# Keys and values of two elements by three float32r products, with the context split where it is turned and kept in DRAM

## The chip, the cores and the metric

The kernel runs on one NeuronCore of a Trainium2 chip. The metric is the device time of one execution in microseconds (us): before the change 1100.62 us, the median of three runs between 1100.51 and 1100.92.

## The reference, cut to what matters

The input is `x`, four elements of 512 tokens with 512 channels, and a context `ctx_2048` of the same shape. Four gated layers are applied in turn:

```
x = x + tanh(g_xattn[0]) * wkv(w, u, k=layernorm(x), v=ctx)          # a recurrence along the tokens
x = x + tanh(g_ffn[0])   * ffn(layernorm(x), w1, w2, w3)             # 1-bit weights, 8-bit activations
x = x + tanh(g_xattn[1]) * attention(layernorm(x), cond=ctx)         # 16 heads of 32
x = x + tanh(g_ffn[1])   * ternary_linear(layernorm(x), gamma, W)
```

In the attention, queries and output go through products of 8-bit integers, but keys and values do not:

```
kv   = cond @ wkv.T + bkv          # float32: 512 tokens x 512 channels, 1024 outputs, for each element
k, v = split(kv, 2)
attn = softmax(q k^T / sqrt(32));  o = attn v
```

They depend on the context and the weights alone, so they can be made for all four elements at any time before the attention.

## The kernel before, in words

**Stages.** One function, `tile_flamingo_kernel`, unrolls everything. A first part (the pools "boot" and "boot_ps") loads and prepares all weights while it runs the recurrence (`wkv_layer`, L554) and the FFN (`ffn_layer`, L694) of the first element; after about 320 us a second part runs the FFN, attention and ternary layer of the elements against each other. All that the change edits runs in the first part, or moves buffers of it.

**Order.** Generators yield after each piece of work. `line(gen, (start, end, steps), ...)` gives each generator places along an axis, `event` a single place, and `run` (L1192) always takes the generator whose next place is lowest. In the first part, `at_us(us)` counts microseconds up to 88, and `at_unit(n)` counts the sixteen (tile of 128 tokens, quarter of the hidden layer) units of the first element's FFN; four steps of `ffn_layer` make one unit. These places set the order in which the program is traced. Every TensorE instruction also gets an order edge behind the last TensorE instruction of the step before (`in_turn`, L147, `next_turn`, L156), so TensorE runs the steps in exactly this order. Instructions of the other engines and the DMA issues are ordered by the framework's planner, which takes the earliest in program order whose operands and buffers are ready by its own estimate of times. Each engine then runs its queue in order. All DMAs here are issued by SyncE (SP).

**Buffers.** A tile pool has a number of buffers for each tag; a tile of a tag waits until a buffer's former tile has been read for the last time. In the first part PSUM has two banks of tag "m" (512 float32 columns each; transposes, and the keys and values of elements one to three beyond the first few), two of "hp" (FFN up products) and four of "acc". In SBUF, tag "k_half" has two buffers, "wn" (raw weights and raw context) two, "cT" one.

**Keys and values** (class `Context`, L439). `weights` and `weights_turned` (L497) fetch the two halves of `wkv` and turn them into `wkvT`, 128 x 4 x 1024 float32. `fetch(b)` (L458) brings the context of element b, `load(b)` (L473) transposes it on TensorE in tiles of 128 tokens (`ct_ps`), copies it on ScalarE into `cT`, and for the third and fourth element stores `cT` to DRAM (`cD`, L484), from where the recurrence reads it later. `keys_values(b, tag)` (L503) makes eight groups: four key groups (128 outputs x 512 tokens: four float32 matmuls over the channel blocks into one bank), each followed by `split` (L247: ScalarE writes the float32r rounding plus bias, VectorE the rest) and a store to `kD` (L520); and four value groups (128 tokens x 512 outputs), each followed by an addition of the bias on VectorE (L535) and a store to `vD` (L537). For the third element the groups stand at units 3.8 to 9.6, for the fourth at 10 to 16; the raw context of the fourth is fetched at unit 9.0 and turned at 9.75.

**FFN unit.** `up` makes eight float32r matmuls of 512 columns into an "hp" bank (twice a unit), `gate` (tanh, L737; L738) and `gated` (L742) and `quantised` (L663) use ScalarE, VectorE and GpSimd, `gate_parts` transposes the result and splits it into float32r parts (`parts`, L682, with L688 on ScalarE and L689 on VectorE), and `down` makes eight more matmuls. Between these steps come the transposes of FFN weights (`turned`, L334) and, from unit 11, the rounding and turning of `wq`, `wp`, `wf` (L368 to L423) into `wqT`, `wpT`, `wfT`.

All matmuls are recorded with line L162 and all transposes with L165, the helpers' lines; the tile's name tells which is which.

## Time and profile before

| | |
|---|---|
| median of three runs | 1100.62 us |
| profiled execution | 1100.92 us |
| its span on the core | 1099.1 us, mean granted TensorE clock 0.963 |
| TensorE busy (matmul) | 939.7 us, 85% |
| VectorE | 831.4 us, 76% |
| ScalarE | 726.0 us, 66% |
| GpSimd | 314.1 us, 29% |
| DMA | 189.68 MB, mean 173 GB/s |

The profile is of one execution. Times of instructions are counted from the start of the span. "Busy" of TensorE counts records of matmuls, which overlap one another, so the cost of one matmul in a row of them is the distance from start to start and not its recorded length. In the groups of instructions, "out<-in" are the program's names, then come partitions x elements and the count, then the total busy time, the mean of one in ns, and the idle time before them with what ended it. In the order of time, a line has start, length, engine, line, operation, names and count, and in brackets the idle time before it and what ended that. SPq is the issuing of DMAs on SyncE.

### The profile page before, as it was taken

To read this page: it belongs to the slowest core of one execution; us is meant where nothing else is said; L and a number is where in the kernel's file an instruction comes from. 1 tells how busy PE (TensorE), PEld (TensorE's weight loads), DVE (VectorE), ACT (ScalarE), POOL (GpSimd) and SP (SyncE) were. 2 spreads that over 40 slices of the span, in tenths; PEclk is the share of its full clock that TensorE was granted. 3 is DMA by queue.
4 is the path that set the end of the run, shared out by engine and by line. 5 is a ranking of instruction groups with operands and counts; after the bars stand their busy time and mean duration, and the time that the engine had idled before them with its cause. 6 is when DMAs were issued, how large, how long until landed. Compare 5 with 4: busy or idle time off the path is not lost.

```text
span 1099.1 us, 17965 instructions
## 1 busy us (share of the span) xinstructions
PE 939.7 (85%) x6380; PEld 678.8 (62%) x6380; DVE 831.4 (76%) x1600; ACT 726.0 (66%) x1490; POOL 314.1 (29%) x311
## 2 busy tenths in 40 slices
PE   4879997998888878889998787999998999878885
PEld 2335564565557666667776465777777777656652
DVE  4976548757676789997669988877697765679977
ACT  6656755567345676667767667677685666977863
POOL 3831104422323153531215546422123321100000
PEclk8889999999998999999999999999999999989998
DMA  8178945454344673744755544566455653343411
GB/s 287 39 257 326 323 170 187 147 216 171 136 134 148 233 234 112 252 134 144 230 190 189 168 164 145 172 216 187 173 200 169 208 192 106 83 149 107 116 49 39
DMA packets 85674, 189.68 MB, mean 173 GB/s; under 512 B 12241, under 2 KB 36817, under 8 KB 74577
## 3 DMA queue, kind: packets, MB, share of 16 engines
q1 hardware_dynamic: 85584, 188.53, 51.6%
q8 instruction: 51, 0.84, 0.3%
q14 instruction: 39, 0.31, 0.1%
HBM read 148.65 MB, written 39.85 MB: 171 GB/s over the span
## 4 chain that ended last, share of the span: by engine, by line
PE 45%; DVE 24%; ACT 15%; POOL 7%; issue 7%; DMA 2%; SPq 0%; POOLq 0%; ACTq 0%; DVEq 0%
PE ff_hp L162 14%; PE ff_acc L162 6%; PE pt_ps L165 5%; PE o_ps L162 4%; PE s_ps L162 4%; ACT at_P L941 3%; DVE wk_q L632 3%; PE v_ps L162 3%; ACT at_PT L961 2%; DVE at_nm L939 2%; PE k_ps L162 2%; PE tp_ps L165 2%; DVE wk_p L626 2%; PE qr_ps L165 2%; DVE qg_i L672 1%
## 5 line engine op out<-in xcount | busy, mean ns | idle before, releaser
L162 PE MATMUL ff_hp<-wT,xp 128*128 128x512 f32 x1024 | 270.0, 407 | 3.8 <-ACT at_P L941 2.1
L162 PEld LDWEIGHTS ff_hp<-wT,xp 128*128 128x128 f32 x1024 | 194.2, 193 | 51.3 <-ACT at_P L941 3.8
L941 ACT ACTIVATE at_P<-s_ps,at_nm 128x512 f32<-128x512 f32 x256 | 174.4, 689 | 73.9 <-DVE at_nm L939 70.0
L939 DVE TENSOR_REDUCE at_nm<-s_ps 128x1 f32<-128x512 f32 x256 | 165.5, 676 | 38.0 <-PE s_ps L162 37.3
L677 POOL TENSOR_TENSOR ff_z<-qg_b,qg_s 128x512 f32<-128x512 bf16 x64 | 71.8, 1121 | 334.4 <-ACT qg_b L676 308.3
L165 PE MATMUL pt_ps<-ident,at_P 128*128 128x128 f32 x1024 | 141.1, 278 | 16.4 <-ACT at_os L981 5.4
L961 ACT COPY at_PT<-pt_ps 128x512 f32<-128x512 f32 x224 | 124.3, 595 | 39.6 <-PE pt_ps L165 38.5
L162 PE MATMUL ff_acc<-wT,hr 128*128 128x512 f32 x512 | 137.3, 409 | 4.8 <-ACT hr L688 3.0
L165 PEld LDWEIGHTS pt_ps<-ident,at_P 128*128 128x128 f32 x1024 | 113.2, 140 | 44.4 <-issue 9.1
L162 PE MATMUL s_ps<-at_kR,at_qR 128*128 128x512 f32 x256 | 97.8, 450 | 22.0 <-ACT at_P L941 14.6
L162 PEld LDWEIGHTS ff_acc<-wT,hr 128*128 128x128 f32 x512 | 92.7, 190 | 25.8 <-ACT hr L688 4.0
L737 ACT ACTIVATE ff_z<-ff_hp,coef 128x512 f32<-128x512 f32 x64 | 44.0, 687 | 46.9 <-PE ff_hp L162 44.3
L162 PE MATMUL o_ps<-at_PT,at_V 128*32 128x128 f32 x2048 | 72.2, 279 | 1.3 <-DVE hr L689 0.7
L676 ACT CAST qg_b<-qg_i 128x512 bf16<-128x512 int8 x80 | 49.3, 617 | 31.3 <-DVE qg_i L672 27.4
L742 DVE SCALAR_TENSOR_TENSOR ff_z<-ff_hp,coef,ff_z 128x512 f32<-128x512 f32 x64 | 47.6, 743 | 29.1 <-PE ff_hp L162 29.1
L162 PEld LDWEIGHTS s_ps<-at_kR,at_qR 128*128 128x128 f32 x256 | 45.6, 193 | 38.8 <-ACT at_P L941 23.7
L162 PEld LDWEIGHTS o_ps<-at_PT,at_V 128*32 128x32 f32 x2048 | 53.8, 111 | 23.8 <-issue 11.3
L738 DVE SCALAR_TENSOR_TENSOR ff_z<-ff_z,ff_hp 128x512 f32<-128x512 f32 x64 | 43.4, 678 | 31.4 <-ACT ff_z L737 29.5
L162 PE MATMUL v_ps<-wkvT,cT 128*128 128x512 f32 x128 | 60.9, 622 | 5.7 <-DVE wT L295 2.3
L162 PE MATMUL k_ps<-cT,wkvT 128*128 128x512 f32 x128 | 61.4, 631 | 2.3 <-ACT wk_k L576 1.0
L165 PE MATMUL tp_ps<-ident,ff_z 128*128 128x128 f32 x256 | 40.3, 281 | 23.2 <-ACT at_PT L961 11.0
L632 DVE RECIPROCAL wk_q<-wk_q 128x256 f32<-128x256 f32 x32 | 54.3, 1718 | 1.4 <-POOL wk_p L620 1.4
(178 smaller groups left out, 1664.3 us busy)
## 6 DMA issues: line engine op xcount, KB each, us to landing
wT<-wD SPq DMA_DIRECT2D x72, 1024.0 KB, 5.3
wn<-in_L_ffn_w_dram SPq DMA_DIRECT2D x18, 1024.0 KB, 7.2
at_kR<-kD SPq DMA_DIRECT2D x128, 128.0 KB, 3.0
at_qR<-qD SPq DMA_DIRECT2D x256, 64.0 KB, 2.3
wD<-wT SPq DMA_DIRECT2D x12, 1024.0 KB, 4.2
kD<-k_half SPq DMA_DIRECT2D x16, 512.0 KB, 2.8
qD<-at_half SPq DMA_DIRECT2D x32, 256.0 KB, 2.1
cn<-in_ctx_dram SPq DMA_DIRECT2D x8, 512.0 KB, 6.0
```

Of the source, the lines that this page charges most:

```text
L162: return in_turn(nc.tensor.matmul(*args, **kwargs))
L165: return in_turn(nc.tensor.transpose(*args))
L626: nc.vector.tensor_tensor_scan(p[:, 1:], A2, E2, 0.0, ALU.mult, ALU.add)
L632: nc.vector.reciprocal(half, half)
L676: nc.scalar.copy(qb, qi)
L677: nc.gpsimd.tensor_tensor(grouped(src), grouped(qb), s.unsqueeze(2).to_broadcast([P, NG, GS]), ALU.mult)
L737: nc.scalar.activation(z, hp, AF.Tanh, scale=coef[:, 0:1])
L738: nc.vector.scalar_tensor_tensor(z, z, 1.0, hp, ALU.add, ALU.mult)
L742: nc.vector.scalar_tensor_tensor(z, hp, coef[:, 1:2], z, ALU.mult, ALU.mult)
L939: nc.vector.tensor_reduce(nm, sp, AX.X, ALU.max, negate=True)
L941: nc.scalar.activation(lanes[k, i, t], sp, AF.Exp, bias=nm, accum_out=sums[k][:, t, i : i + 1],)
L961: made[k] = nc.scalar.copy(dst, blocks(pt))
```

## The change

For the third and fourth element, a float32 product of two float32 matrices becomes three float32r products of their parts (high x high, high x low, low x high).

- Each tile of 128 context tokens of these elements, when turned, is also written as a float32r high part (ScalarE) and the remainder (VectorE) into `c_both` (tag "k_half"), both from the same PSUM bank, and stored to DRAM (`cS`). `load` now yields after each tile. `cD` is still written.
- The weights are held as two tiles `W[0]` (keys) and `W[1]` (values). Before the new products, `split_weights` splits them: low parts into buffers whose later owners (`wqT`, `wpT`, `wfT`, `bp_b`, `swp_b`) are now allocated when they are made, high parts into two "k_half" buffers and from there by DMA over the place of `W`.
- Keys and values of these two elements are made in four halves of 256 tokens. `fetch_half` brings both parts of half a context into one buffer of tag "cT"; `half_keys_values` makes two key banks (each with two output blocks of 256 columns, 12 matmuls and one `split` a block) and two value banks (12 matmuls of 512 columns each).
- Places: element four's context is fetched at unit 3.0 (before: 9.0) and turned from 3.5 (9.75); weights are split at 3.8 and 4.6; the halves run at 5.4 to 6.6, 7.2 to 8.4, 9.0 to 10.2 and 10.8 to 12.0, each fetched 0.58 unit ahead.

The first and second element keep the float32 products. The core of the diff:

```diff
@@ class Context, load @@
             for t in range(NT):
-                self.transposed(cT[:, :, t * P : (t + 1) * P], self.cn[b][t // 2][:, t % 2, :])
+                cut = slice(t * P, (t + 1) * P)
+                pt = self.transposed(cT[:, :, cut], self.cn[b][t // 2][:, t % 2, :])
+                if b > 1:
+                    both = self.pool.tile([P, 2, D], F32R, name="c_both", tag="k_half", bufs=2)
+                    nc.scalar.copy(both[:, 0, :], pt)
+                    nc.vector.tensor_tensor(
+                        both[:, 1, :], pt, both[:, 0, :].bitcast(F32), ALU.subtract
+                    )
+                    for i in range(2):
+                        nc.sync.dma_start(
+                            out=cS[b][i, :, :, cut], in_=blocks(both[:, i, :]).bitcast(F32)
+                        )
+                yield
@@ new in class Context @@
+        def split_weights(self, i):
+            W = self.W[i]
+            high = [
+                self.pool.tile([P, 2, D], F32R, name="w_hi", tag="k_half", bufs=2)
+                for _ in range(2)
+            ]
+            for c in range(NC):
+                tag = (("wqT", "wpT"), ("wfT", ("bp_b", "swp_b")))[i][c // 2]
...
+                hi = high[c // 2][:, c % 2, :]
+                nc.scalar.copy(hi, W[:, c, :])
+                nc.vector.tensor_tensor(lo, W[:, c, :], hi.bitcast(F32), ALU.subtract)
+                self.low[i, c] = lo
+                if c % 2:
+                    yield
+            self.W[i] = self.pool.tile([P, NC, D], F32R, name="w_high", tag=f"wkvT{i}")
+            for h in range(2):
+                nc.sync.dma_start(
+                    out=self.W[i][:, 2 * h : 2 * h + 2, :].bitcast(F32),
+                    in_=high[h].bitcast(F32),
+                )
+
+        def fetch_half(self, b, h):
+            self.pair = self.pool.tile([P, 2, NC, 2 * P], F32R, name="c_pair", tag="cT")
+            cut = slice(2 * P * h, 2 * P * (h + 1))
+            for i in range(2):
+                nc.sync.dma_start(
+                    out=self.pair[:, i].bitcast(F32), in_=cS[b][i, :, :, cut]
+                )
+
+        def half_keys_values(self, b, h):
...
+            def products(out, c, w, ctx):
+                i, w = w.start // D, slice(w.start % D, w.start % D + w.stop - w.start)
+                high = self.W[i][:, c, w], ctx(hi)
+                low = self.low[i, c][:, w], ctx(lo)
+                for n, (x, y) in enumerate(((0, 0), (0, 1), (1, 0))):
+                    weight, context = (high, low)[x][0], (high, low)[y][1]
+                    pair = (context, weight) if i else (weight, context)
+                    matmul(
+                        out,
+                        lhsT=pair[0],
+                        rhs=pair[1],
+                        start=(c == 0 and n == 0),
+                        stop=(c == NC - 1 and n == 2),
+                    )
+
+            for g2 in range(0, NC, 2):
+                kp = psum_tile("k_ps", "m")
+                half = self.pool.tile([P, 2, 2, 2 * P], F32R, name="k_half", tag="k_half", bufs=2)
+                for g in (g2, g2 + 1):
+                    out = kp[:, (g - g2) * 2 * P : (g - g2 + 1) * 2 * P]
+                    for c in range(NC):
+                        products(out, c, slice(g * P, (g + 1) * P), lambda a: a[:, c, :])
+                    split(half[:, g - g2], out, self.bkc[:, g : g + 1])
+                store()
...
+                yield
+            for j in range(2):
+                t = 2 * h + j
+                vp = psum_tile("v_ps", "m")
+                for c in range(NC):
+                    products(vp, c, slice(D, 2 * D), lambda a: a[:, c, j * P : (j + 1) * P])
+                V = self.pool.tile([P, D], F32, name="V", tag="k_half", bufs=2)
+                nc.vector.tensor_tensor(V, vp, self.bv_b, ALU.add)
...
@@ the places @@
-        for b, load, over, start in ((2, 0.7, 2.0, 3.6), (3, 9.0, 9.75, 9.8)):
+        for b, load, over in ((2, 0.7, 2.0), (3, 3.0, 3.5)):
             event(at_unit(load), lambda b=b: context.fetch(b))
-            event(at_unit(over), lambda b=b: context.load(b))
+            line(late(lambda b=b: context.load(b)), (at_unit(over), at_unit(over + 0.4), 4))
+        for i, start in enumerate((3.8, 4.6)):
             line(
-                late(lambda b=b: context.keys_values(b, "m")),
-                (at_unit(start + 0.2), at_unit(start + 6.0), 8),
+                late(lambda i=i: context.split_weights(i)),
+                (at_unit(start), at_unit(start + 0.4), 3),
+            )
+        for b, h, start, end in (
+            (2, 0, 5.4, 6.6),
+            (2, 1, 7.2, 8.4),
+            (3, 0, 9.0, 10.2),
+            (3, 1, 10.8, 12.0),
+        ):
+            event(at_unit(start - 0.58), lambda b=b, h=h: context.fetch_half(b, h))
+            line(
+                late(lambda b=b, h=h: context.half_keys_values(b, h)),
+                (at_unit(start), at_unit(end), 4),
             )
```

## The prediction

> **What bounds the kernel now.** I read the page's list of groups first, to see what a key or value product costs beside a float32r product, then the stage in which the edited work runs, by windows, then the waits of TensorE in that stage, then the order of time at single places. The stage is that of the first element's FFN, in which everything that the change touches is placed: about 101 us (first ff_hp) to 317 us, sixteen units of 13.5 us.
>
> ```profile
> L162 PE MATMUL ff_hp<-wT,xp 128*128 128x512 f32 x1024 | 270.0, 407 | 3.8 <-ACT at_P L941 2.1
> ...
> L162 PE MATMUL v_ps<-wkvT,cT 128*128 128x512 f32 x128 | 60.9, 622 | 5.7 <-DVE wT L295 2.3
> L162 PE MATMUL k_ps<-cT,wkvT 128*128 128x512 f32 x128 | 61.4, 631 | 2.3 <-ACT wk_k L576 1.0
> ```
>
> The program issues 16 key and value groups of four products for each of four elements, 256 products, and 256 records are here: 128 of each kind for 64 products. So one float32 product is two records. What a product costs is not its mean (records overlap) but the distance between starts, which the order of time gives:
>
> ```profile
> 115.80 2.07 PE L162 MATMUL ff_hp<-wT,xp 128*128 128x512 f32 x8
> ...
> 123.78 0.59 PE L162 MATMUL v_ps<-wkvT,cT 128*128 128x512 f32 x1
> 124.21 0.60 PE L165 MATMUL ct_ps<-ident,cn 128*128 128x128 f32 x4
> 124.41 0.69 DVE L535 TENSOR_TENSOR V<-v_ps,gamma_b 128x512 f32<-128x512 f32 x1 [2.96 <-PE v_ps L162]
> 125.16 1.09 PE L165 MATMUL ct_ps<-ident,cn 128*128 128x128 f32 x8 [0.35 <-DVE V L535]
> ...
> 133.74 3.59 PE L162 MATMUL v_ps<-wkvT,cT 128*128 128x512 f32 x8
> ```
>
> A group of v_ps is 3.59 us with the end of its last record: (3.59 - 0.59)/7 = 0.429 us a record, 0.857 us a float32 product, 3.43 us a group. For float32r, (2.07 - 0.40)/7 = 0.238 us a product of 512 columns. Transposes of 128 columns come (1.09 - 0.33)/7 = 0.109 us apart. The lines also show the wait that matters below: ct_ps stands until DVE has read the bank that it wants, and TensorE restarts 0.06 us after DVE's end.
>
> ```profile
> 101.00:317.00 216.00, 190.41 (x862) 123.84 (x861) 140.85 (x237) 128.05 (x205) 55.63 (x55) 0.98 0.53 190
> 263.00:276.50 13.50, 11.76 (x62) 7.67 (x61) 10.16 (x18) 13.16 (x23) 1.39 (x2) 1.00 0.79 289
> ```
>
> ```profile
> PE wt_ps L165 <- DVE k_half L250: 5.0, 2, 4.0
> PE wt_ps L165 <- DVE V L535: 3.9, 3, 2.7
> PE v_ps L162 <- DVE wT L295: 2.3, 2, 2.1
> ```
>
> Columns of the windows (first fence; the second is TensorE's waits in the stage: in total, times, longest): PE, PEld, DVE, ACT and POOL busy, granted clock, DMA share, GB/s. TensorE is busy 190.4 of 216 us (88%) at clock 0.98, DVE 65%, ACT 59%: TensorE bounds the stage. Its largest waits, five of the kind above, are for a PSUM bank that ACT or DVE has yet to read: the stage has two of tag "m" for all transposes, keys and values.
>
> **The change, part by part.**
>
> *Products.* Removed: 16 groups (elements three and four) x 3.43 = 54.9 us of TensorE. Added: values, 4 halves x 2 x 4 x 3 = 96 float32r products of 512 columns x 0.238 = 22.8 us; keys, 4 x 4 x 4 x 3 = 192 of 256 columns. No 256-column float32r product is in the trace. Below it is 0.109 (128 columns), above 0.238 (512). Half of 0.238 is 0.119, the straight line between the two rows gives 0.152; I take 0.130, between them and nearer the halving, since the 0.109 of the transposes is about a weight load (two came 0.108 us apart), not columns. Keys: 25.0 us (20.9 to 45.7). Sum 47.8: **-7.1 us** (-11.2 to +13.6).
>
> The row first: 0.238 us at 512 columns. The Trainium skill, TensorE: Matmul & The Clock Gate, section Back-to-back issue gap, gives N/2.4 + 2.5 ns, 216 ns at 512 columns and 109 at 256; the measurement is 10% above it. By the page the keys would take 20.9 us and the term would be -11.2.
>
> *Two key blocks in one bank.* Now each half puts two blocks of 256 columns into one PSUM tile, and the first is split (ACT, then DVE) before the second's products. No row has TensorE writing one half of a bank while another engine reads the other, so the bounds are nothing and the full wait (a wait can't gain). All of TensorE's waits on eviction in the rows are for a whole tile, so I take the full wait. It is: the last product's tail 0.40 - 0.24 = 0.16; 0.04 to start ACT (the DVE line above starts 0.04 after v_ps); ACT on 256 columns, 0.47 (L249's 0.68 at 512, less the 0.21 by which a copy falls from 0.58 at 512 to a midpoint of 0.37 with at_os's 0.27 at 128); 0.05; DVE 0.43 (line between 0.28, at_o at 128, and 0.72, L250); 0.06 to restart: 1.2 us. ACT and DVE are busy 59% and 65% with instructions of 0.7 us: half of one, in that share of cases, is 0.2 + 0.2 more: 1.6. There are 2 such pairs a half, 8 in all: **+13 us** (0 to +16). Nothing on TensorE can pass, as turns are chained: behind it queue the FFN's up and down products, and ACT and DVE wait for those.
>
> On the same point the Trainium skill, PSUM — Partial Sum Buffer, section PSUM bank collisions raise a hardware error, tells to guard by bank, not by address, disjoint columns included; no run here shows it yet, and it speaks against this change.
>
> *Loads of elements three and four.* Per tile of 128 tokens ACT gains a copy (0.59, as L688) and DVE a subtraction (0.68, as L689); the bank is held through both, 1.3 us longer. c_both has two buffers, each held by ACT, DVE, two SP issues of 0.32 and a landing (256 KB: vD<-V 2.5, at_V<-vD in 512-byte runs 4.1): 5 to 6 us, where the tiles come some 1.4 us apart. Tiles three and four wait about 2 to 3 us for a buffer with their bank held, and TensorE's next transposes stand. Per load 2 us (0 to 6): **+4 us** (0 to +12). Eight copies (4.7 us) and eight subtractions (5.4) lie otherwise beside TensorE, in ACT's and DVE's idle 41% and 35%; without that cover they would cost 10.
>
> *Queues.* SP gets 16 cS writes, 8 pair fetches, 4 weight copies, 8 more key stores: 36 issues x 0.36 = 13 us, of 216, in a queue that mostly waits (for L250 alone 68 us). The two cn fetches of element four and its cD write move from unit 9-10 to 3-4, past weight loads on SP, and take a "wn" buffer that the load of (0,2) would have had, which then comes half a unit later, about its 6.0 us landing before its use: part of the +1 below. DMA is 0.93 busy at 128-141.5 and 0.65 in the next unit, and gets about 5 MB there. POOL is passed by none of these.
>
> *Weight splits.* 8 ACT copies (0.6) and 8 DVE subtractions (0.68), no bank: hidden in the same idle shares; with slower loads **+1 us** (0 to 5). The lower parts live in the buffers of wqT, wpT, wfT, bp_b, swp_b, which are wanted from unit 12.6 and last read by 12.0: nothing, if the halves keep time. Fetches of halves: 512 KB took 5.1 us (cn); the single pair buffer leaves 0.58 unit = 7.8 us: nothing; if late by its full landing, 5 us a half. Key evictions, 16 + 16 of 256 columns for 8 + 8 of 512, +2.1 us ACT and +1.1 DVE, lie in the waits counted.
>
> *What moves.* Key and value work now ends at unit 12. In unit 12-13 (second window line) ACT is busy 13.2 of 13.5 us, so with 3.65 us of products gone it stays 13 us long: TensorE idles, **+2** (0 to 5). The windows of units 5-12 (168.5 to 263) add up to 12.9 us of TensorE idle; denser products, and the eight waits, let ACT and DVE catch up: half goes, **-6.5** (-10 to -3).
>
> Sum: -7.1 + 13 + 4 + 1 + 2 - 6.5 = +6.4. The profiled execution took 1100.92 (span 1099.1 and 1.8 around it), 0.3 above the median of 1100.62, so 1107.3 against it, 1107.0 against the median. After 320 us nothing is edited; 0.2% (2.2 us) is about what a measurement can tell from no change.
>
> **Rivals.**
> *No wait inside the bank* (ends faster): if TensorE may write columns 256-511 while ACT reads 0-255, or the waits take only time that TensorE lost anyway, 13 goes to 0 and the catching up to -3: -7.1 + 0 + 4 + 1 + 2 - 3 = -3.1, 1097.5; with the cheapest product 1093. For it: idle TensorE time exists (25.6 us). Against: each wait on a bank in the rows lasts till its last reader. It decides when a wait costs under 0.8 us net.
> *256 columns cost nearly as much as 512*: weight loads bound them; at 0.19 us the keys take 36.5, +11.5: 1118.5. For: float32r weight loads are recorded at 190 ns, transposes' at 140. Against: they overlap (0.108 apart).
> *The c_both buffers bind*: DMA at 0.9 makes landings 6 to 8 us (cD 7.0), each load costs 6: +8, 1115.
> *The stage is not the measure*: TensorE's gain and loss cancel in ACT- and DVE-bound stretches: 1098.5 to 1102.8.
>
> **How the numbers follow.** Forecast with its bounds, 1103 to 1112: 0.50. Slow product or buffers, 1112 to 1122: 0.15. Cancelling: 0.12. No wait in the bank, 1092 to 1098.4: 0.23. So slower 0.65, same 0.12, faster 0.23. Range 1094 to 1119, leaving out about 0.05 below and 0.08 above; the forecast's own is 1103 to 1112.
>
> **What would show it.** The distance of k_ps starts (0.13 at 256 columns); eight waits PE k_ps <- DVE k_half of 1 us or more, about 10 to 13 us together, where there were none; waits of ACT c_both on its DMA near 125-165 us and PE ct_ps behind; units 5.4 to 12 longer, the last four shorter; first ff_hp of the second element some 6 us later. Wrong if k_ps shows no such wait, or if the stage's TensorE idle does not grow.

## The result, and the profile after

The changed kernel takes 1134.56 us (median of four runs, 1134.38 to 1135.76); beside it the kernel before took 1100.77 (1100.51 to 1101.92). The ratio is 1.031, with a 95% interval of 1.0297 to 1.0326: 34 us slower, where the prediction had 1107.0 and a range up to 1119. The direction was right, the size was not.

First, from the groups of instructions by line and shape of the kernel after, the new key products with the high parts of the weights, of 256 columns (busy us and mean ns of one; idle time before them and what ended it).

```profile
L159 PE MATMUL k_ps<-c_pair,w_high 128*128 128x256 f32 x128 | 28.9, 320 | 28.1 <-DVE k_half L247 18.8 <-ACT w_hi L537 6.1 <-DMA c_pair<-cS 2.5
```

Half of the float32 records are gone, as announced: 64 each of k_ps and v_ps, with 33.0 and 31.9 us busy, are left of 128. But the line of the new key products has nearly as much idle time in front of it (28.1 us) as work in it, and two thirds of that is named k_half, the wait inside the bank.

Now windows of the same kernel after (PE, PEld, DVE, ACT and POOL busy, granted TensorE clock, DMA share, GB/s). The first line is the stage from the first ff_hp of the first element to the first ff_hp of the second. The others are stretches of it: the load of the third element, the 3.4 us before the longest stretch at half clock, and that stretch, from the weight splits into the first half.

```profile
100.74:367.68 266.94, 204.39 (x1069) 156.02 (x1069) 170.22 (x296) 144.42 (x238) 64.17 (x64) 0.91 0.60 205
128.00:141.50 13.50, 8.88 (x36) 6.78 (x36) 5.68 (x10) 5.86 (x9) 0.00 (x0) 0.75 0.60 177
175.80:179.20 3.40, 1.18 (x9) 0.65 (x7) 2.66 (x4) 1.11 (x2) 1.36 (x2) 1.00 1.10 423
179.20:199.70 20.50, 7.89 (x29) 6.95 (x30) 16.66 (x18) 7.69 (x13) 10.38 (x10) 0.50 0.54 181
```

The same stage of the kernel before:

```profile
100.99:332.89 231.90, 201.24 (x909) 131.40 (x908) 153.78 (x271) 133.51 (x215) 63.64 (x64) 0.98 0.54 190
```

The whole loss lies in this stage: 266.9 us instead of 231.9, +35.0. TensorE is busy 3.1 us longer and idle 62.6 us instead of 30.7, so 31.9 of the 35.0 us are idle time. Its work did not shrink in time because it ran at a lower clock: the granted clock is 0.91 instead of 0.98, so (1 - 0.91) x 266.9 = 24 us of full clock are missing, where before it was (1 - 0.98) x 231.9 = 5. Not all of that is lost time, since TensorE also stands in the slow stretches: in the one from 179.2 to 199.7 it is busy for 7.89 of 20.5 us. By the count of the products its busy time should be 8.2 us shorter (worked out further below), and it is 3.1 longer, so the lower clock costs some 11 us of busy time, an estimate. ACT has 10.9 us more work in the stage and DVE 16.4.

Where in the stage: the start of the same ff_hp matmul in both traces.

| start before (us) | 116.1 | 139.9 | 153.5 | 181.4 | 223.4 | 270.4 | 315.6 | 341.6 |
|---|---|---|---|---|---|---|---|---|
| later after by | -0.3 | 6.7 | 12.6 | 29.4 | 30.0 | 44.1 | 35.2 | 33.6 |

7.0 us are added at the load of the third element, 5.9 at that of the fourth, 17 at the weight splits and the first half, 14 at the last two halves; some 10 are won back in the last four units, and little changes after 341.6. The lags also carry products that were moved. Of the 17 us, 14.3 are idle time of TensorE; but of the 14, 9.3 are busy time, as two halves' products stand where four float32 groups stood; and what is won back comes from four value groups, 13.7 us, that have left the last units. TensorE's largest waits in the stretch from 88 to 360 us of the kernel after:

```profile
PE k_ps L159 <- DVE k_half L247: 18.8, 8, 7.9
PE tp_ps L162 <- DVE c_both L492: 6.5, 2, 4.6
PE k_ps L159 <- ACT w_hi L537: 6.1, 1, 6.1
PE wt_ps L162 <- DVE hr L800: 5.0, 4, 3.3
PE k_ps L159 <- DMA c_pair<-cS: 2.5, 4, 1.1
```

Eight waits on the first block's split were announced, and eight are there. But they range up to 7.9 us. The order of time of the kernel after shows the longest of them and the wait ahead of it (POOL, loads of weights and some other lines are left out):

```profile
175.85 2.52 SPq L554 DMA_DIRECT2D c_pair<-cS  x2
...
176.58 0.40 PE L162 MATMUL wt_ps<-identb,sg 128*128 128x128 bf16 x4
...
183.11 0.55 PE L159 MATMUL k_ps<-c_pair,w_high 128*128 128x256 f32 x1 [6.14 <-ACT w_hi L537]
...
187.92 0.47 ACT L246 ACTIVATE k_half<-k_ps,bkc 128x256 fp32r<-128x256 f32 x1 [1.86 <-DMA w_high<-w_hi]
...
189.19 2.27 DVE L737 TENSOR_TENSOR_SCAN wk_p<-wk_e 128x512 f32<-128x512 f32 x1 [1.15 <-POOL wk_e L733]
...
191.38 3.33 DVE L743 RECIPROCAL wk_q<-wk_q 128x256 f32<-128x256 f32 x2
...
194.64 0.38 DVE L247 SCALAR_TENSOR_TENSOR k_half<-k_ps,bkc,k_half 128x256 fp32r<-128x256 f32 x1
...
195.07 0.79 PE L159 MATMUL k_ps<-c_pair,w_high 128*128 128x256 f32 x2 [7.95 <-DVE k_half L247]
...
200.74 0.48 PE L159 MATMUL k_ps<-c_pair,w_high 128*128 128x256 f32 x2
...
202.11 0.28 PE L159 MATMUL k_ps<-c_pair,w_lo 128*128 128x256 f32 x1
```

From 176.98 to 183.11 TensorE stands before the first key product, whose context parts were asked for from 175.85 on, behind two weight copies on SP. The profile puts this wait down to w_hi, which the product doesn't read; the two c_pair transfers land 7.3 us after their issue (median, by the profile's DMA issues of 165 to 215 us), and 175.85 + 7.3 = 183.15, which fits the end of the wait (from 175.8 to 179.2 the DMA share is 1.10). The wait that ends at 195.07 has two parts. ACT's half of the split waits 1.86 us for a k_half buffer that a weight copy still reads, 0.8 us of it after the end of the last product at 187.12. Then DVE, which needs 0.38 us for its half, first runs a scan of the recurrence, for whose operand it stands until 189.19, and two reciprocals (2.27 + 3.33 us) that stand ahead of it in its queue. TensorE goes on 0.43 us after the split's start. The last two lines carry the price of a product: twelve start between 200.74 and 202.11, (202.11 - 200.74)/11 = 0.1245 us apart. The first distance is longer than the others; the last ten, from 201.06 on, are 0.117 us apart.

### The profile page after: what moved, and what is told of

It is laid out like the page before. It is cut to its first block, busy times and chain, and to the rows that moved or that the text cites. A ratio compares the mean times of both kernels' runs of the same rounds, so it can differ in the third digit from the quotient of the medians.

```text
span 1134.0 us, 18402 instructions
## 1 busy us (share of the span) xinstructions
PE 940.2 (83%) x6510; PEld 703.6 (62%) x6540; DVE 848.6 (75%) x1624; ACT 737.1 (65%) x1514; POOL 314.4 (28%) x311
## 4 chain that ended last, share of the span: by engine, by line
PE 44%; DVE 22%; ACT 14%; issue 7%; POOL 7%; DMA 5%; SPq 0%; ACTq 0%; POOLq 0%; DVEq 0%
PE ff_hp L159 13%; PE ff_acc L159 6%; PE pt_ps L162 5%; PE o_ps L159 4%; PE v_ps L159 3%; PE s_ps L159 3%; ACT at_P L1052 3%; PE k_ps L159 3%; DVE at_nm L1050 2%; DVE wk_q L743 2%; ACT at_PT L1072 2%; PE tp_ps L162 2%; DVE qg_i L783 1%; ACT wk_e L715 1%; DVE wk_p L737 1%
## 5 line engine op out<-in xcount | busy, mean ns | idle before, releaser
L159 PE MATMUL ff_hp<-wT,xp 128*128 128x512 f32 x1024 | 273.7, 411 | 2.8 <-ACT at_P L1052 2.1
L159 PEld LDWEIGHTS ff_hp<-wT,xp 128*128 128x128 f32 x1024 | 198.5, 198 | 48.5 <-ACT at_P L1052 3.8
L159 PEld LDWEIGHTS o_ps<-at_PT,at_V 128*32 128x32 f32 x2048 | 53.4, 110 | 22.8 <-issue 10.5
L799 ACT CAST hr<-tp_ps 128x512 fp32r<-128x512 f32 x64 | 37.6, 588 | 22.9 <-PE tp_ps L162 22.5
L159 PE MATMUL k_ps<-c_pair,w_high 128*128 128x256 f32 x128 | 28.9, 320 | 28.1 <-DVE k_half L247 18.8
```

What stands on the lines that cost most here:

```text
L159: return in_turn(nc.tensor.matmul(*args, **kwargs))
L799: nc.scalar.copy(part[:, 0, :], pt)
```

## The experiments

The theory after this reading had four parts: the waits inside the bank cost about 10 us net; the loads cost 11 to 12 instead of 4; the first half comes late through SP's queue and the k_half buffers; and pauses halve the clock. The rival was that the stage has become bound by something else, so that the removal of one wait only shows the next. Each ratio is taken to the kernel before on the same chip, whose median there was 1099.95 to 1101.68 us; differences in us between kernels carry this spread.

### Waits inside the bank

> The changed kernel, with both key blocks of a bank multiplied before either is split. Theory (the second block's products wait in TensorE's order for the split of the first, and the split's VectorE half stands behind the recurrence's scans and reciprocals): the eight waits of k_ps on k_half, 18.8 us, go, and the time falls by 14 to 20 us from 1134.6, to 1115 to 1121. Rival (TensorE would have stood there anyway, since VectorE is late in these units): the idle time turns up before other transposes and products, and the time stays above 1129.

```diff
                     for c in range(NC):
                         products(out, c, slice(g * P, (g + 1) * P), lambda a: a[:, c, :])
+                for g in (g2, g2 + 1):
+                    out = kp[:, (g - g2) * 2 * P : (g - g2 + 1) * 2 * P]
                     split(half[:, g - g2], out, self.bkc[:, g : g + 1])
```

With both blocks multiplied before both splits: 1124.31 us (1123.65 to 1129.31), ratio to before 1.0221 (1.0187 to 1.0255). 10.2 us come back of the 18.8 us of these waits. Its waits from 88 to 360 us:

```profile
PE k_ps L159 <- DMA c_pair<-cS: 9.0, 3, 6.7
PE wt_ps L162 <- DVE hr L802: 8.5, 6, 3.3
PE k_ps L159 <- DVE k_half L247: 7.8, 1, 7.8
```

Seven of the eight waits are gone, 11.0 us, and the waits for hr are 3.5 us longer. The row of c_pair is longer by name only: its longest, 6.7, is the wait before the first key product, 6.1 in the changed kernel and there put down to w_hi, so it is 9.0 instead of 2.5 + 6.1 = 8.6. That the same wait has c_pair's name here speaks for the reading above. The other way to shorten the same waits is to leave them and to put the recurrence's scans, product and reciprocals behind a split that was traced before them:

> The changed kernel, with an order edge: the recurrence's scans, products and reciprocals on VectorE that are traced after a split stand behind that split's VectorE half. Nothing else is changed, the two blocks still share a bank. Theory (the long waits inside a bank are the recurrence's instructions ahead of the split in VectorE's queue): the 18.8 us of k_ps on k_half fall to 9 to 11 us (eight waits of some 1.2), and the time falls by 6 to 12 us from 1134.6, to 1122 to 1129. Rival (the recurrence is itself what the stage waits for, so that it is late instead): less than 3 us.

```diff
+        return nc.vector.scalar_tensor_tensor(
...
+                    lows.append(split(half[:, g - g2], out, self.bkc[:, g : g + 1]))
...
+            after_split(nc.vector.tensor_tensor_scan(q[:, 1:], A2, E2, 0.0, ALU.mult, ALU.add))
```

1130.72 us (1129.73 to 1133.11), ratio 1.0279 (1.0261 to 1.0297); before on that chip was 1099.95.

```profile
PE k_ps L159 <- DVE k_half L255: 10.9, 8, 2.4
PE k_ps L159 <- DMA c_pair<-cS: 9.1, 4, 6.5
...
PE k_ps L159 <- ACT wT L298: 3.4, 1, 3.4
```

The eight waits fall from 18.8 to 10.9 us and the longest from 7.9 to 2.4: so about 8 us of them were DVE's queue, and at most 1.4 us each (10.9/8) the wait itself, near the 1.6 of the prediction. But the kernel gains 3.8 us, not 8. The wait before the first key product is the same, 6.5 us, and again put down to c_pair. Other waits grow: the largest is one of 3.4 us for wT before a k_ps, where the changed kernel has 0.7.

### Where the halves and the weights stand

Three edits move the same work: the halves and their fetches one unit later; the first fetch earlier, ahead of the weight copies on SP; the weights' splits earlier, at units 0.6 and 4.0.

> The changed kernel, with all four halves and their fetches one unit later (6.4 to 13.0). Theory (the first half comes before its fetch and its split weights are there: one wait of 6.1 us and one of 0.75, with the clock at half afterwards): the wait before the first k_ps goes, and the time falls by 6 to 10 us, to 1125 to 1129; the eight waits of k_ps on k_half stay, in sum 10 to 20 us. Rival (the long waits follow from where the recurrence's instructions stand, wherever the halves are): same within 3 us.

> The changed kernel, with the first half's fetch placed at unit 3.75 (4.82), ahead of the weights' copies in SP's queue. Theory (SP stands 6.6 us at the first weight copy until VectorE has made the low part, and the fetch behind it lands only at 183 to 184 us): the 6.1 us wait before the first k_ps goes and the time falls by 4 to 7 us, to 1128 to 1131. Rival (ScalarE's split of the weights or the clock set the start of the first half): within 2 us.

> The changed kernel, with the key weights split at unit 0.6 (3.8) and the value weights at 4.0 (4.6). Theory (the weights' high parts hold both k_half buffers until their copies have landed, so that ScalarE stands at the first half's split and TensorE behind it): the 6.1 us wait before the first k_ps and the long wait (7.9 us) in the first half shrink, and the time falls by 6 to 14 us from 1134.6, to 1121 to 1128. Rival (the long waits are the recurrence's instructions ahead in VectorE's queue, or the fetch of the first half): same within 3 us.

```diff
-            (2, 0, 5.4, 6.6),
+            (2, 0, 6.4, 7.6),
...
-            event(at_unit(start - 0.58), lambda b=b, h=h: context.fetch_half(b, h))
+            event(at_unit(3.75 if start == 5.4 else start - 0.58), lambda b=b, h=h: context.fetch_half(b, h))
...
-        for i, start in enumerate((3.8, 4.6)):
+        for i, start in enumerate((0.6, 4.0)):
```

Each line of the diff was one kernel (the first with the other three halves moved alike): 1133.88 (1133.05 to 1135.07), 1139.07 (1137.17 to 1141.3) and 1142.7 us (1141.82 to 1144.33), ratios 1.0299 (1.0272 to 1.0326), 1.0353 (1.0334 to 1.0372) and 1.0376 (1.0359 to 1.0393). One changes nothing, two are slower. The theory that SP's queue or the weights' k_half buffers alone make the price of the first half fell. Where the pair is fetched first, TensorE starts the first key block 1.6 us earlier (181.46 instead of 183.11), but then its split stands 14.2 us: ACT waits 7.33 us for the k_half buffer of a weight copy, and DVE has the weights' subtractions, scans and two reciprocals ahead of its half. Its waits of this kind from 100 to 360 us:

```profile
PE k_ps L159 <- DVE k_half L247: 22.8, 8, 14.2
```

### The price of the loads

To the kernel before were added only the loads' new work, at the places that the change gives them as far as the rest of that kernel allows (units 2.0 and 9.45, in four steps); nothing reads it.

> The kernel before, with c_both made and stored for elements three and four as in the change (four steps from unit 2.0 and from 9.45), read by nothing; products as before. Theory (the price of the loads is their own, some 6 us each while DMA is at 0.85, less at unit 9.5): slower than before by 7 to 13 us, 1108 to 1114. Rival (the lag seen at the loads is only taken from slack and comes back by the end of the stage): within 3 us of the kernel before.

```diff
+                pt = self.transposed(cT[:, :, cut], self.cn[b][t // 2][:, t % 2, :])
+                if b > 1:
+                    both = self.pool.tile([P, 2, D], F32R, name="c_both", tag="k_half", bufs=2)
+                    nc.scalar.copy(both[:, 0, :], pt)
+                    nc.vector.tensor_tensor(
+                        both[:, 1, :], pt, both[:, 0, :].bitcast(F32), ALU.subtract
+                    )
+                    for i in range(2):
+                        nc.sync.dma_start(
+                            out=cS[b][i, :, :, cut], in_=blocks(both[:, i, :]).bitcast(F32)
+                        )
+                yield
```

1112.24 us (1109.75 to 1113.71), ratio 1.0095 (1.0075 to 1.0115): +10.9 us with no product changed. Two variants took the operands from the copy in SBUF, not from the PSUM bank, once here and once in the changed kernel:

> The kernel before with the loads split (as in the run of the loads alone, 10.9 us slower than before), but with c_both from the copy in SBUF. Theory (the price of the loads is the PSUM bank held while c_both waits for a buffer): 2 to 5 us slower than before, 1103 to 1106. Rival (it is ScalarE and SP standing in their queues, or DMA): 8 us or more.

> The changed kernel, with c_both made from the copy in SBUF (cT) and not from the PSUM bank, so that the bank is free after ScalarE's first copy. Theory (the two banks held while c_both waits for a buffer cost TensorE the 6.7 us of lag at the third element's load and most of the 6 us at the fourth's): the wait of tp_ps on c_both (6.5 us) goes and the time falls by 8 to 13 us, to 1121 to 1127. Rival (ScalarE itself stands in its queue at c_both until a buffer's store has landed, and all behind it stands too): it falls by less than 4.

```diff
-                    nc.scalar.copy(both[:, 0, :], pt)
+                    nc.scalar.copy(blocks(both[:, 0, :]), cT[:, :, cut])
```

Added to the kernel before: 1111.74 (1105.84 to 1113.35), ratio 1.0094 (1.0063 to 1.0125), the same price. In the changed kernel: 1130.24 (1129.47 to 1132.69), ratio 1.0269 (1.024 to 1.0297), 4.3 less than without. In the changed kernel what comes back is speed: in its stage of 260.2 us TensorE's idle time is nearly the same, 61.9 us instead of 62.6, and its busy time 6 us shorter. In the kernel before, the bank held longer is not what makes the loads' price. The order of time of the first of these two, at the third element's load (DVE, PEld and SP left out), shows what does:

```profile
132.17 0.62 ACT L487 CAST c_both<-cT 128x512 fp32r<-128x512 f32 x1 [2.90 <-DMA cS<-c_both]
...
132.69 0.58 ACT L294 CAST wT<-wt_ps 128x512 fp32r<-128x512 bf16 x1
...
133.32 0.38 PE L166 MATMUL wt_ps<-identb,sg 128*128 128x128 bf16 x4 [2.19 <-ACT wT L294]
```

ACT's third copy waits 2.90 us for a buffer that a transfer still reads. Behind it in ACT's queue stands the copy of turned FFN weights, and TensorE waits 2.19 us for that; the eight ff_acc matmuls after it, from 133.52 on, take 3.46 us, where they take 2.09 at full clock. The next three kernels take that price apart: the steps alone, the transfers alone (from `cT`; the diff is this kernel against the one with all of it), and the copies and subtractions alone.

> The kernel before with the two loads only cut into four steps and the second of them begun 0.3 unit earlier, as in the three kernels before this one: no split, no transfer. It is the zero of that comparison. If the order of the steps alone costs nothing, it is within 2 us of before; what it takes more than before is to be subtracted from the other two.

> The kernel before, with the two transfers to cS per tile of the third and fourth element issued at the places of the loads, but taken from cT itself: no copy, no subtraction, no c_both buffer. The kernel with the loads' whole new work took 10.9 us more than before, and the same with the operands taken out of SBUF 10.4. If the transfers make that price (16 more issues on the SyncE queue, 4 MB more when the DMA engines are 0.93 busy), this takes 8 to 11 us more than before. If the copies and subtractions make it, it takes 0 to 3 us more, and TensorE's waits on c_both are gone.

> The same kernel with the copy and the subtraction into c_both out of the PSUM bank, but without the transfers to cS: nothing reads c_both. If ACT's and DVE's instructions and the bank held for them make the price, this takes 8 to 11 us more than before and TensorE's waits on c_both stay (7.8 us with the transfers). If it is the transfers that hold the c_both buffers, 1 to 4 us, and those waits go to under 2 us.

```diff
-                    both = self.pool.tile([P, 2, D], F32R, name="c_both", tag="k_half", bufs=2)
-                    nc.scalar.copy(both[:, 0, :], pt)
...
-                            out=cS[b][i, :, :, cut], in_=blocks(both[:, i, :]).bitcast(F32)
+                            out=cS[b][i, :, :, cut], in_=cT[:, :, cut]
```

| added to the kernel before | median us (range) | ratio to before, 95% |
|---|---|---|
| steps alone | 1100.43 (1098.64 to 1104.13) | 0.9992 (0.9978 to 1.0006) |
| transfers alone | 1100.58 (1099.04 to 1103.63) | 0.9988 (0.9974 to 1.0002) |
| copies and subtractions alone | 1107.62 (1107.01 to 1108.64) | 1.0048 (1.0033 to 1.0063) |
| all of it | 1112.24 (1109.75 to 1113.71) | 1.0095 (1.0075 to 1.0115) |

The transfers cost nothing by themselves. Eight copies and eight subtractions cost 0.48%, 5.3 us, between the two expectations. All together cost 10.4 to 10.9: the other five appear only when the transfers hold the two buffers that the copies want. TensorE's waits on c_both were 3.2 us in three without transfers and 9.8 in four (longest 4.8) with them, in the kernel that takes the operands from the bank. What the 5.3 us consist of, two orders of time show, at the fourth element's load. The kernel with the steps alone:

```profile
229.24 1.20 PE L166 MATMUL ct_ps<-ident,cn 128*128 128x128 f32 x8 [0.41 <-DVE xb L649]
...
231.44 3.63 PE L163 MATMUL k_ps<-cT,wkvT 128*128 128x512 f32 x8
234.51 2.41 PE L163 MATMUL ff_hp<-wT,xp 128*128 128x512 f32 x8
```

And with the copies and subtractions alone:

```profile
229.73 0.66 PE L166 MATMUL ct_ps<-ident,cn 128*128 128x128 f32 x4 [0.45 <-DVE xb L655]
231.93 1.11 PE L166 MATMUL ct_ps<-ident,cn 128*128 128x128 f32 x4 [1.54 <-DVE c_both L488]
233.00 1.09 PE L166 MATMUL tp_ps<-ident,ff_z 128*128 128x128 f32 x4
234.93 5.60 PE L163 MATMUL k_ps<-cT,wkvT 128*128 128x512 f32 x8 [0.85 <-DVE c_both L488]
239.97 2.41 PE L163 MATMUL ff_hp<-wT,xp 128*128 128x512 f32 x8
```

From the first line to the ff_hp it is 10.24 us instead of 5.27. The waits are 2.84 us instead of 0.94 (0.53 of it at a tp_ps left out here), 1.9 more. The rest is speed: the same k_ps group takes 5.60 instead of 3.63, and four transposes of 128 columns 1.1 instead of 0.63. Windows of this kernel just before and at that place, and its stage (columns as above; the clock is the third number from the end):

```profile
228.60:232.00 3.40, 1.40 (x12) 0.93 (x11) 1.76 (x3) 3.40 (x7) 1.04 (x1) 0.99 0.74 308
...
232.00:238.80 6.80, 5.95 (x13) 3.15 (x14) 1.98 (x3) 6.46 (x12) 0.10 (x1) 0.50 0.53 145
...
99.44:337.04 237.60, 207.15 (x909) 134.03 (x908) 161.87 (x279) 138.06 (x223) 63.68 (x64) 0.95 0.53 183
```

The same three of the kernel with the steps alone, whose clock stayed at 1.00:

```profile
228.60:232.00 3.40, 2.46 (x17) 1.65 (x15) 0.58 (x1) 3.40 (x8) 1.04 (x1) 1.00 0.51 207
...
232.00:238.80 6.80, 6.80 (x28) 4.16 (x26) 2.45 (x3) 6.80 (x13) 0.10 (x1) 1.00 0.91 299
...
100.17:331.80 231.63, 201.18 (x910) 131.76 (x909) 153.94 (x271) 133.31 (x215) 63.59 (x64) 0.98 0.54 190
```

In the 3.4 us before 232.0 TensorE is busy for 1.40 us in the first and 2.46 in the second, and the next 6.8 us are at half clock in the first alone. Over the stage it is 6.0 us longer, and TensorE's idle time is the same: 237.60 - 207.15 = 30.45 and 231.63 - 201.18 = 30.45. All 6.0 us are busy time of an unchanged set of instructions, at a clock of 0.95 instead of 0.98: 0.03 x 237.6 = 7 us. (The execution profiled with the steps alone took 1104.13 us in all, 3.7 above the median, but its stage is as long as that of the kernel before, 231.9.)

### All causes at once, and what remains

> The three edits together. If the three costs are separate and add up, 28 to 40 us come back and the time is 1095 to 1107, near or under the kernel before. If they are one lack of slack that shows at three places, less comes back than the three alone give in sum: 1110 or more.

The three edits (both blocks before the splits, operands out of SBUF, halves one unit later) give 1116.29 us (1114.95 to 1116.72), ratio 1.0139 (1.0108 to 1.0171): 18.3 us less than the changed kernel, where each alone gives 10.2, 4.3 and 0.7. Neither expectation fits: it is less than 28, but not less than the 15.2 that the three give alone in sum. Two more combinations did no better: these three with the weights' early split, and the first two with the recurrence behind and the first fetch early.

> Both blocks before both splits, c_both from SBUF, halves one unit later, and the weights split at 0.6 and 4.0. Against the 1116.3 us without the last edit: if the buffers held by the weights are what is left at the first half (ScalarE stood 9.9 us there), 8 to 14 us less, 1102 to 1108; if the added 14 us of VectorE and 10 us of ScalarE work bind in units 5 to 12, less than 4 us, 1112 or more.

> Together: both blocks before both splits, c_both from SBUF, the recurrence behind the splits, the first fetch ahead of the weights' copies; places of the halves as in the change. Against 1116.3 us for the earlier combination (with later halves): if VectorE's and SP's order make what was left, 8 to 14 us less, 1102 to 1108; if the added work on VectorE and ScalarE does, 1112 or more.

1117.13 (1115.16 to 1124.75), ratio 1.0155 (1.0117 to 1.0193); and 1119.74 (1114.2 to 1122.15), ratio 1.0167 (1.0131 to 1.0204). The best kernel that computes the reference stays 16 us behind the one before. Its largest wait between 100 and 360 us is of another kind than those of the changed kernel:

```profile
PE wt_ps L162 <- DVE wT L292: 9.9, 3, 5.7
```

It is for banks of turned FFN weights that DVE has yet to copy; then come c_pair with 4.0 us and the same banks by ACT with 3.7, and k_half has 1.8 left. Whether TensorE's work still matters in such a stage, two kernels with one product of three tell:

> The changed kernel with high x high alone: 192 of the 288 products are left out (the results lack the low parts' share), all else stays. That is some 31 us of TensorE (16 us of 256-column and 15 us of 512-column products). If the stage is still bound by TensorE's work, the time falls by 25 to 31 us, to 1104 to 1110. If it is bound by waits for ScalarE, VectorE and buffers, most of this turns into idle time: it falls by 15 or less, to 1120 or more.

> The changed kernel with the three edits (both blocks of a bank multiplied before the splits, the operands of the loads out of SBUF, the halves one unit later), which took 1116.3, and with the products of the high parts alone: 192 of the 288 float32r products are left out, 31 us of TensorE, and the results lack the low parts' share. If what remains of the loss is TensorE's work at its clock, this takes 20 to 31 us less, 1085 to 1096, under the kernel before. If ACT, DVE, the queues and the pauses bound the stage, it takes 0 to 8 us less, 1108 to 1116: then no saving of products can pay in this place.

```diff
-                for n, (x, y) in enumerate(((0, 0), (0, 1), (1, 0))):
+                for n, (x, y) in enumerate(((0, 0),)):
```

Left out are 192 of 288 float32r products, 128 x 0.1245 + 64 x 0.238 = 31 us. The changed kernel without them takes 1120.89 (1119.06 to 1122.89), ratio 1.0179 (1.0156 to 1.0202): 13.7 less. The one with three edits takes 1093.85 (1092.12 to 1096.74), ratio 0.9917 (0.9898 to 0.9935): 22.4 less. With the waits in place, less than half of the TensorE time that is taken away arrives at the end; with the three edits, nearly three quarters. In the first of these kernels the waits grow as the products shrink: the eight on k_half are 23.7 us, not 18.8.

The expectation for the second had 1085 to 1096 if TensorE's work is what remains, and 1108 to 1116 if ACT, DVE and pauses do; the time lies in the first. So ACT and DVE don't set a floor at 1116: where the waits are thinned out, TensorE's work counts again. Two last kernels leave the splits out, on top of the three edits, so that a low part is the whole value again:

> The changed kernel with the three edits (both blocks of a bank multiplied before the splits, the operands of the loads out of SBUF, the halves one unit later), 1116.3, and with both parts in DRAM written from cT itself, which the transfers alone have shown to cost nothing: ctx is not split, its low part is the whole again, and the results are off by that. Copies, subtractions and their two buffers cost 5 to 11 us when added to the kernel before. If they cost as much inside the changed kernel, this takes 5 to 11 us less, 1105 to 1111. If the loss is elsewhere by then, 0 to 3 less.

> The same, and the weights are not split either: both parts come from W by transfers, no copy and subtraction by ACT and DVE, no k_half buffers held by them, no copies back. Only the 288 products, the halves' fetches and their splits are left of the change. If the weights' split costs little (the sum had +1), this is within 3 us of the kernel with the loads' split alone left out. If it holds ACT, DVE and the buffers ahead of the first half, as the lag there suggests, it takes 5 or more less. What is left above the kernel before, minus the 7.1 which the products should save, is the price of the halves.

```diff
-                    nc.scalar.copy(blocks(both[:, 0, :]), cT[:, :, cut])
...
-                            out=cS[b][i, :, :, cut], in_=blocks(both[:, i, :]).bitcast(F32)
+                            out=cS[b][i, :, :, cut], in_=cT[:, :, cut]
...
-                nc.scalar.copy(hi, W[:, c, :])
-                nc.vector.tensor_tensor(lo, W[:, c, :], hi.bitcast(F32), ALU.subtract)
+                nc.sync.dma_start(out=lo.bitcast(F32), in_=W[:, c, :])
```

Without the loads' splits: 1107.74 us (1106.76 to 1107.96), ratio 1.0068 (1.0053 to 1.0083), 8.6 less, so the loads' price is about the same inside the changed kernel as alone. Without the weights' splits as well (second part of the diff) it is 1114.59, with one run at 1107.07 and three between 1114.42 and 1115.29, ratio 1.0112 (1.0073 to 1.0152): no gain, and eight transfers into the low parts' places came in. It doesn't tell what the weights' splits cost; that stays open.

So the 34 us are divided as 18.3 (three edits) + 8.6 (loads' splits) + 7.4 (what the first of these two kernels stands above before) = 34.3. The sum closes by itself, since each term is the step from one kernel to the next; what a term holds depends on the order of the steps. As the products should save 8 by their count, the last 7.4 hold some 15 us, an estimate, for the halves and the weights together, their fetches, splits, stores and the clock; the runs don't divide them further.

## Why the prediction was right and wrong

The sum had +6.4 and 34 were measured. By size, the miss lies in the halves and weight splits (some 15 us by the estimate above, where the sum had +1), in the catching up (-6.5, of which nothing is seen) and in the loads (10.9 instead of 4).

**Products, -7.1: right.** The mechanism and the size hold: 0.1245 us for 256 columns where the sum took 0.130, so 192 x 0.1245 + 22.8 = 46.7 us are added for 54.9 removed, -8.2. The rival in which 256 columns cost nearly as much as 512 falls. The page's 0.109 (the Trainium skill, TensorE: Matmul & The Clock Gate, Back-to-back issue gap) was 12% below this mean and 7% below the 0.117 of the later products, as it is 9% below at 512. These prices are at full clock; in the stage the saving didn't arrive, as busy time rose by 3.1. Nor did the step see that TensorE's time is worth its full length only where TensorE isn't waiting; here 13.7 of 31 us.

**Two key blocks in one bank, +13: right in kind, mis-sized in its terms.** Eight waits, all by DVE's half of the split. They are 18.8 us, 2.35 each instead of 1.6. The bare wait is at most 1.4, by the kernel with the recurrence behind the splits; the other 8 us are the DVE queue, for which the step had 0.2 + 0.2 from a busy share. A share of 65% says nothing on which instruction stands ahead: it was a scan of 2.27 and two reciprocals of 1.67. With seven of them gone, 11.0 us, the kernel is 10.2 faster; with 7.9 us of the queue gone it is 3.8 faster, since other waits grow. The rival without any wait in the bank falls.

**Loads, +4: mis-sized, +10.9 measured.** The bounds of 0 to 12 held it, the value taken did not. Two things were wrong. "Eight copies (4.7 us) and eight subtractions (5.4) lie otherwise beside TensorE, in ACT's and DVE's idle 41% and 35%": they cost 5.3 us by themselves, half of the 10 that the text gave for them without that cover, and what they cost is busy time of TensorE at half clock. And the c_both buffers, which the text did see, cost five more as soon as transfers hold them; the rival "the c_both buffers bind" (6 us a load) had the loads' price nearly right, with 1115 in all still 20 us short, as it changed nothing else.

**Queues, splits and halves, "nothing, if the halves keep time": wrong.** They don't keep time. From 153.5 to 181.4 of the time before, the lag goes from 12.6 to 29.4 us, 14.3 of it idle time (the first half's waits inside its banks are among it). What is late next depends on the place: c_pair, the k_half buffer that a weight copy holds, DVE's recurrence. None of the moves tried alone gained over 1 us; two lost 5 and 8. That SP is "a queue that mostly waits" was no cover: the first pair was asked for at 175.85, when TensorE was 1.1 us from standing.

**Catching up, -6.5: wrong.** The idle time of the stage doubled, 30.7 to 62.6 us. The new work on ACT (+10.9) and DVE (+16.4) sits in the same units as the waits; that this left nothing with which to catch up is likely, but no run shows it alone.

**Unit 12 to 16, +2: about right.** Behind the last half the lag falls from 44.1 to 35.2 us at 315.6, but the four value groups that leave this stretch are 13.7 us. TensorE's busy time there falls from 38.8 to 27.0 us, and its idle time grows from 6.3 to 9.2, 2.9 us of the saving that don't arrive.

**What the sum lacked altogether: the granted clock.** 24 us of full clock are missing in the stage instead of 5, which costs some 11 us of busy time by the estimate above. No term stood for it, although every term that adds a pause can add it. Which part of a measured cost is clock was shown only for the copies and subtractions alone, where the whole lengthening of the stage is busy time, and for the operands out of SBUF, where nearly the whole gain is.

## What to carry to other kernels

An instruction that is put on ACT or DVE between two TensorE steps is to be priced by what stands ahead of it in that engine's queue and who waits for it, not by the engine's mean idle share: with 35 to 41% idle, eight copies and eight subtractions cost 5 us. Where TensorE follows a fixed order, a pause can also halve the clock of the work behind it and cost more than it lasts: 1.9 us of waits took 3.1 more in that way. And a wait that is one of several in a row should be removed alone and with the others before it is given a price: here removals of 10, 4 and 1 us made 18 together, and others only moved the wait.

## What the runs showed of the hardware

The granted clock fell to one half in whole stretches, and short waits were enough. In the changed kernel it was 0.50, among others, from 131.4 to 138.3, 158.7 to 165.6 and 179.2 to 199.7 us: 6.9, 6.9 and 20.5 us, two, two and six times 3.4. The order of time of the kernel after, at the third element's load:

```profile
131.33 1.12 ACT L491 CAST c_both<-ct_ps 128x512 fp32r<-128x512 f32 x2 [2.64 <-DMA cS<-c_both]
...
132.70 1.12 PE L162 MATMUL tp_ps<-ident,ff_xn 128*128 128x128 f32 x4 [4.62 <-DVE c_both L492]
...
133.46 3.76 PE L159 MATMUL ff_hp<-wT,xp 128*128 128x512 f32 x8
```

ACT waits for a buffer that a transfer holds, TensorE stands 4.62 us for DVE, and then eight matmuls that take 2.10 us elsewhere take 3.76. In the kernel with copies and subtractions alone, waits of 0.45 and 1.54 us among transposes had the same effect for 6.8 us. The Trainium skill, TensorE: Matmul & The Clock Gate, Part 1: The HAM clock gate, says that the clock is halved after an idle window of 3.4 us and released after a busy one, the windows running free of the program; the lengths of the stretches agree. But the 3.4 us ahead of a stretch weren't idle here: TensorE was busy for 1.18 of them before 179.2 and for 1.40 before 232.0 in the kernel with copies and subtractions alone, while with 2.46 the clock stayed; the measurement decides, and from which busy share on it falls was not measured. The page puts the ramp, by which it means the first 3.4 us of work at half clock, under 1% of a typical kernel's span; here the clock falls again and again, and that costs some 11 us of busy time in this stage by the estimate above, 1.0% of 1134.

Not expected was also that 2 MB of further transfers an element cost nothing where the DMA engines were 0.93 busy already. The window of the third element's load in the kernel before:

```profile
128.00:141.50 13.50, 12.76 (x69) 8.60 (x68) 6.96 (x12) 8.63 (x16) 1.04 (x1) 1.00 0.93 328
```

And in the kernel with the transfers alone:

```profile
128.00:141.50 13.50, 12.53 (x65) 8.44 (x64) 6.36 (x11) 9.33 (x18) 1.04 (x1) 1.00 1.05 352
```

A DMA share of 1.05, and TensorE 12.53 of 13.5 us busy at full clock. What no run showed is TensorE writing one half of a bank while another engine reads the other: both orders tried keep these apart.
